# Stage 1's last addition moved to VectorE in iterations with side work, and a changed order of the last outputs and stores

## The chip, the cores and the metric

The kernel runs on one core of a Trainium2 chip. The metric is the device time of one execution in microseconds (us); a comparison uses the median of several runs. Every time in this document is in us unless it is marked ns.

A core has five engines that run their own instruction streams in order and meet through semaphores: TensorE (PE; its weight loads are listed apart as PEld), VectorE (DVE), ScalarE (ACT), GpSimd (POOL) and SyncE (SP). SP does no arithmetic; it issues DMAs, as ScalarE can too.

## The reference

The input `x` has 128 samples of 64 channels and 1024 positions, in float32; `cond_512` holds a style vector of 128 numbers for each sample. Four convolution layers (three taps, 64 to 64 channels) run one after the other, and the result is added to `x`. The weights of every layer are scaled for each sample.

```python
TYPES = ('same', 'upsample', 'same', 'downsample')
...
s = style @ mw.T + mb
weight = SCALE * w * s[:, None, :, None]
demod = lax.rsqrt(jnp.sum(weight * weight, axis=(2, 3)) + EPS)
weight = weight * demod[:, :, None, None]
...
if typ == 'same':
    out = jax.vmap(_conv_same)(x, weight) + b[None, :, None]
elif typ == 'upsample':
    out = jax.vmap(_conv_up)(x, weight.transpose(0, 2, 1, 3)) + b[None, :, None]
    out = _blur(out, 2.0 * blur_k, (1, 1))
elif typ == 'downsample':
    xb = _blur(x, blur_k, (2, 2))
    out = jax.vmap(_conv_down)(xb, weight) + b[None, :, None]
...
x = x + out
```

There is no nonlinear step between the layers, so the four of them are one linear map for each sample.

## The kernel before, in words

The kernel uses that linearity. For each sample it multiplies the weights of the four layers and the blur kernels into one combined kernel, and then convolves `x` once with it. The few positions at both ends of a row, where padding makes the combined kernel wrong, are computed layer by layer in small pieces ("ends").

**Tiling.** Four samples make one quad `q`; 32 quads are the 32 iterations of the main loop (line 1101). 64 channels of two samples fill the 128 partitions, and every matrix product is made of 64 by 64 quarters.

**The weight chain of a quad** has three stages, spread over the iterations ahead of the quad's convolution. In iteration `q` the loop works on four quads at once: outputs of `q`, convolution of `n = q+1`, stages 2 and 3 of `c = q+2`, stage 1 of `s = q+3`.
- Stage 1 multiplies layers 4 and 3 into the tile `S` (six slots of 64 columns for each half). `stage1_a` makes the first matmuls and lets ScalarE copy four slots (L411, shown as L340 of the helper `scaled_copy`). `stage1_b` makes two more groups of matmuls, lets VectorE form slots 4 and 5 (two `scalar_tensor_tensor`, L422), and adds slot 0 onto slot 2 with one `tensor_add` on GpSimd (L425). That addition reads only slots which ScalarE has written.
- Stage 2 multiplies `S` with layer 2 and the blur (`E`), 36 products, L439. Its first four products read slots 1 to 3 of `S`, so they need the addition; slots 4 and 5 are read by the next four.
- Stage 3 multiplies in layer 1 (L480). VectorE then forms sums of the taps (`H`, L501 in the helper `sum_of`).

**The convolution** is done in a form with five products (conv0 to conv4, L590). VectorE forms differences of the input planes (`G` with L501, `T` with L550 and L577), and GpSimd two more (`T`, L565 and L570, 128x684 each). VectorE's `sum1` (the tile `y`) stands ahead of conv2, and its `sum2` (the tile `Y`, then `y`, L641) ahead of the next iteration's conv4. ScalarE writes the outputs (`output`, L659) with a scale and a bias for each half; the six planes of a quad go out by two stores (L664).

**Order.** The schedule is written by hand: the order of the calls in the loop is the order on each engine. An iteration has these calls in this order: stage 2 of `c`; sum2 of `q`; the tap sums of `n`; conv4 of `q`; stage 3 of `c` and conv3 of `n` with the input differences in between; part of conv0; conv1; sum1; the rest of conv0; part of conv2; the rest of conv2; the stores. GpSimd's L565 and L570 for `c` (`in1`, `in2`) stand ahead of sum1.

**Side work.** In iterations 1, 2, 3, 5, 6, 7, 9, 12, 14, 19 and 24 (the dictionary `SLOTS`, L1031) a group of matmuls for the ends or for per-sample constants takes the place at which stage 1 otherwise begins. Stage 1 of `s` is then pushed back: `stage1_a` to where `stage1_b` otherwise stands, and `stage1_b` behind the first part of conv2 (L1206). In those iterations only the second and third part of conv2 lie on PE between `stage1_b` and the next iteration's stage 2. The side work's vector operations (`extra`, L1208) stand directly behind `stage1_b`, ahead of the next iteration's sum2. They are on VectorE and GpSimd, and some follow in iterations that have no such matmuls.

**The last iteration** (L1107 to L1119) has only conv4, the outputs and the stores. For each half it writes three planes: plane 2 (from `Y`), plane 1 (from `y`) and plane 0 (from conv0). `BOTH` is the pair ScalarE, VectorE: plane 1 of half 0 is written by ScalarE, that of half 1 by VectorE, and so for plane 0. The four stores are issued by SP in this order: planes 1 and 2 of half 0, of half 1, plane 0 of half 0, of half 1.

Of the kernel before, what the change touches and what calls it, by code (L numbers as in the profile page):

```python
# [55 lines left out]
K = 3  # L56
# [7 lines left out]
def kernel(  # L64
# [9 lines left out]
    nc = tc.nc  # L74
# [8 lines left out]
    nc_v, nc_a, nc_g = nc.vector, nc.scalar, nc.gpsimd  # L83
# [282 lines left out]
    def tap_matmul(ps, wd, at, n, weight, taps, first=False, last=False):  # L366
        for r, rows in enumerate(HALF):
            for c, cols in enumerate(HALF):
                nc.tensor.matmul(  # L369
                    ps[r][cols, at * C : (at + n) * C],  # L370
                    weight[rows],
                    wd[c if r == 0 else 1 - c][rows, taps],
                    start=first,
                    stop=last,
                    skip_group_check=True,
                )
# [34 lines left out]
            scaled_copy(nc_a, flat(st[r][:, :4]), ps[r][:, : 4 * C], tBn[:, q, r : r + 1])  # L411
        chain[q] = wd, ps, st, t

    def stage1_b(q):

        wd, ps, st, t = chain[q]
        tap_matmul(ps, wd, 1, 1, w2n[:, 3, :], slice(3, 4))
        tap_matmul(ps, wd, 3, 1, w2n[:, 4, :], slice(4, 5), last=True)
        for r in range(2):
            p1 = st[r][:, 0:1, :].to_broadcast([P, 2, C])  # L420
            sums = ps[r][:, C : 5 * C].rearrange("c (a b o) -> c a b o", a=2, b=2)[:, :, 0]
            nc_v.scalar_tensor_tensor(  # L422
                st[r][:, 4:, :], sums, tB[:, q, r : r + 1], p1, op0=ALU.mult, op1=ALU.subtract
            )
        nc_g.tensor_add(t[:, :, 2], t[:, :, 2], t[:, :, 0])  # L425
        chain[q] = st

    def stage2(q, pool=None, engs=(nc_a, nc_a), between=None):
        st = chain[q]
        ps = unit(pool or ps_w, f"psR{q}")  # L430
        for n, e in enumerate((-2, -1, 0, 1, 2, 3, 4, 5, 6)):
            if e % 2 == 0:
                a, lo, m = slice(1, 4), e // 2 + 1, 3
            else:
                a, lo, m = slice(4, 6), (e + 3) // 2, 2
            for r, rows in enumerate(HALF):
                for c, cols in enumerate(HALF):
                    src = st[c if r == 0 else 1 - c]
                    nc.tensor.matmul(  # L439
                        ps[r][cols, lo * C : (lo + m) * C],  # L440
                        E[rows, e + 2, :],
                        src[rows, a, :],
                        start=(n == 0),
                        stop=(n == 8),
                        skip_group_check=True,
                    )
        if between:
            between()
        rt = []
        for r in range(2):  # L450
            t = r_pool.tile([P, 7, C], F32, tag="R", name=f"R{q}_{r}")
            scaled_copy(
                engs[r], t.rearrange("c t o -> c (t o)"), ps[r][:, : 7 * C], tC[:, q, r : r + 1]
            )
            rt.append(t)
        chain[q] = rt
        return ps
# [152 lines left out]
    def banks(q):  # L610
        return A[q] if isinstance(A[q], list) else [A[q][:, s] for s in range(2)]
# [24 lines left out]
    def sum2(q):  # L636
        m3 = m3c.pop(q)
        for s, a in parts(q):
            sum_of(Y[:, s, :NB], m3[:, s], 3.0, a)
        for s, a in parts(q):  # L640
            nc_v.tensor_sub(y1w[q][:, s], y1w[q][:, s], a)  # L641

    def conv4(q, *groups):
        product(q, 4, Y_banks, groups or range(K))

    def conv0(q, *groups):
        product(q, 0, banks(q), groups)
# [3 lines left out]
    def output(q, i, s, eng=nc_a):  # L651

        if q not in os:
            os[q] = opool.tile([P, 2, K, NB], F32, tag="o", name=f"o{q}")
        d3, add = td[:, q, s : s + 1], tb[:, q, s : s + 1]
        src = (banks(q)[s][:, :NB], y1w[q][:, s], Y[:, s, :NB])[i]
        dst = os[q][:, s, i]
        if eng is nc_a:
            nc_a.activation(dst, src, AF.Identity, bias=add, scale=d3)  # L659
        else:  # L660
            eng.tensor_scalar(dst, src, d3, add, op0=ALU.mult, op1=ALU.add)

    def store(q, s, planes=slice(0, K)):
        nc.sync.dma_start(  # L664
            out[q, :, s, planes.start * NB : planes.stop * NB],
            os[q][:, s, planes].rearrange("c i j -> c (i j)"),
        )
# [108 lines left out]
    def zeros():  # L776
        for t in Ye:
            nc_g.memset(t[:, :, 0:1], 0.0)
            nc_g.memset(t[:, :, 7:8], 0.0)
        for t in Ue:  # L780
            nc_g.memset(t[:, :, 0:1], 0.0)
            nc_g.memset(t[:, :, 10:11], 0.0)
        for t in Ve:
            nc_g.memset(t[:, :, 0:2], 0.0)
            nc_g.memset(t[:, :, 10:12], 0.0)
        nc_g.memset(g1, 0.0)
# [142 lines left out]
    BOTH = nc_a, nc_v  # L929
# [171 lines left out]
    for q in range(NQ):  # L1101
        n, c, s = q + 1, q + 2, q + 3
        if q == 1:
            nc.sync.dma_start(Xe, x_ends)
        if q == 5:
            zeros()
        if n == NQ:  # L1107
            conv4(q)
            for i in range(2):
                output(q, 2, i)  # L1110
            for i, eng in enumerate(BOTH):
                output(q, 1, i, eng)
            for i in range(2):
                store(q, i, slice(1, 3))
            conv0(q, *range(K))
            for i, eng in enumerate(BOTH):
                output(q, 0, i, eng)
                store(q, i, slice(0, 1))
            break  # L1119
        if c < NQ:  # L1120
            stage2(c)
        if n < NQ - 1:
            sum2(q)
        if n < NQ - 1:
            combine_a(n)
            combine_b(n)

        if n == NQ - 1:

            conv3(n, ps_w)  # L1130
            copy_m3(n)
            conv4(q, 0, 1)
            for i in range(2):
                output(q, 1, i)
            conv1(n)
            sum1(n)
            conv4(q, 2)
            for i in range(2):
                output(q, 2, i)
            in04(n, 0)  # L1140
            in04(n, 1)
            conv0(q, 0)
            conv2(n)
            conv0(q, 1, 2)
            sum2(n)
            for i in range(2):
                output(q, 0, i)
                store(q, i)
            continue

        conv4(q)
        if q == 0:
            var_matmul(PART[1], var_of(PART[1]), start=False)
            var_root(PART[1], var_of(PART[1]))
            var_inverse(PART[1])
            var_newton(PART[1])
            table_A(PART[1], dm[:, 2, PART[1]])
            for of in (table_C, vector_c0, table_3, vector_Da):
                of(PART[1])
        for i in range(2):  # L1160
            output(q, 2, i)
        if c < NQ:
            stage3(c, 0)
        conv3(n)
        copy_m3(n)
        in04(n, 0)
        in04(n, 1)
        if q:
            in3(c)
            in_g01(c, 0)  # L1170
            in_g01(c, 1)
        if c < NQ:
            stage3(c, 1)
        conv0(q, 0)
        conv1(n, 0)
        if q in SLOTS:
            slot(*SLOTS[q])
        elif s < NQ:
            stage1_a(s)
        conv1(n, 1, 2)  # L1180
        for i in range(2):
            output(q, 1, i)
        if q:
            in_g2(c)
            load(c + NX)
        if q and c < NQ - 1:
            in1(c, nc_g)
            in2(c, nc_g)
        if n == NQ - 2:
            combine_a(n + 1, lambda: sum1(n))  # L1190
            combine_b(n + 1)
        else:
            sum1(n)
        if q == 0:
            in_g01(c, 0)
            in_g01(c, 1)
        conv0(q, 1)
        if q in SLOTS:
            stage1_a(s)
        elif s < NQ:  # L1200
            stage1_b(s)
        conv0(q, 2)
        for i in range(2):
            output(q, 0, i)
        conv2(n, 0)
        if q in SLOTS:  # L1206
            stage1_b(s)
        extra(q, 0)  # L1208
        extra(q, 1)
        if s + 1 < NQ:  # L1210
            scale3(s + 1)
        conv2(n, 1, 2)
        if n == NQ - 2:
            sum2(n)
            in1(n + 1, nc_v)
            in2(n + 1, nc_v)
        if q == 0:
            in_g2(c)
            in3(c)
            load(c + NX)  # L1220
            in1(c, nc_g)
            in2(c, nc_g)
        for i in range(2):
            store(q, i)
# [74 lines left out]
```

## Time and profile before

| | |
|---|---|
| median of 3 runs | 495.94 (495.86 to 497.52) |
| span of the profiled execution | 495.3 |
| mean granted TensorE clock | 0.997 |
| GpSimd's L425, 29 times | 447 to 985 ns, median 463 ns |
| VectorE's L422, 58 times | 340 to 353 ns, median 343 ns |
| GpSimd's L565 and L570, 30 times each | 1668 and 1664 ns, mean |
| last four stores, from issue to landing | 3.4 to 4.3 |

How to read the lines that follow in the prediction. A row of the list of waits is "engine, tile and line that waited <- who ended the wait: total time, how often, longest". A row of the timeline is "start, length, engine, line, operation, out<-in, shape, count", and in brackets the engine's idle time before it and what ended it. Engines with a q behind the name are their sequencers, which issue DMAs. A row of the table by windows is the window, its length, the busy time of each engine with the number of its instructions, the granted clock, the share of the 16 DMA engines that were busy, and GB/s. The profile shows VectorE instructions that follow each other overlapping by up to 0.09.

### The profile page before, as it was taken

What the parts mean: (1) busy time and instruction counts of PE and PEld (TensorE: products, weight loads), DVE (VectorE), ACT (ScalarE), POOL (GpSimd) and SP (SyncE); (2) the same over time, 40 slices, a digit from 0 to 9 for tenths busy, and PEclk for the clock granted to TensorE, in tenths of its full rate; (3) what the DMA queues carried; (4) which work ended last, traced back from release to release, by engine and by line L of the source; (5) the groups of instructions that cost most, each with busy time, mean ns of one, the idle gap of its engine ahead of it and who ended that gap; (6) DMA issues with size and microseconds to landing.
All of it is one profiled execution on the core that took longest, in us unless ns stands there. A gap on an engine that the chain in (4) does not pass through costs nothing.

```text
span 495.3 us, 22221 instructions
## 1 busy us (share of the span) xinstructions
PE 481.3 (97%) x10056; PEld 359.4 (73%) x10056; DVE 396.0 (80%) x692; ACT 290.8 (59%) x580; POOL 142.1 (29%) x175
## 2 busy tenths in 40 slices
PE   8999999999999999999999999999999999999994
PEld 6877767766776766767888777767767778888862
DVE  4986987798888869996768897759998768878782
ACT  5366646557565656555566656656555657566552
POOL 3544423435223222123232122222123333211200
PEclk9999999999999999999999999999999999999998
DMA  7220644442334442354433344442344442434224
GB/s 247 95 90 3 219 167 174 172 162 93 118 148 172 174 148 84 118 171 172 173 127 113 119 161 172 174 146 82 124 167 172 172 161 101 155 129 164 88 86 171
DMA packets 19728, 70.42 MB, mean 142 GB/s; under 512 B 2224, under 2 KB 2992, under 8 KB 19632
## 3 DMA queue, kind: packets, MB, share of 16 engines
q1 hardware_dynamic: 19552, 68.87, 39.0%
q8 instruction: 79, 1.29, 1.1%
q14 instruction: 17, 0.14, 0.1%
q10 hardware_dynamic: 80, 0.11, 0.1%
HBM read 35.36 MB, written 33.62 MB: 139 GB/s over the span
## 4 chain that ended last, share of the span: by engine, by line
PE 78%; DVE 13%; POOL 5%; issue 2%; ACT 0%; POOLq 0%; DVEq 0%
PE psA L590 35%; PE psR L439 13%; PE psW L480 12%; PE Y L590 9%; PE psS L369 5%; DVE G L501 3%; DVE H L501 2%; POOL T L565 2%; POOL T L570 2%; PE psE L820 2%; DVE T L577 2%; DVE Y L501 1%; DVE y L641 1%; POOL S L425 1%; DVE Wf L498 1%
## 5 line engine op out<-in xcount | busy, mean ns | idle before, releaser
L590 PE MATMUL psA<-T,H 64*64 64x340 f32 x2304 | 192.5, 446 | 0.7 <-DVE y L501 0.7
L565 POOL TENSOR_TENSOR T<-G 128x684 f32<-128x684 f32 x30 | 50.0, 1668 | 295.3 <-DVE G L501 268.8
L590 PEld LDWEIGHTS psA<-T,H 64*64 64x64 f32 x2304 | 94.3, 133 | 51.5 <-DVE y L501 5.6
L439 PE MATMUL psR<-S,E 64*64 64x192 f32 (+1 forms) x2304 | 88.1, 300 | 4.7 <-POOL S L425 4.0
L439 PEld LDWEIGHTS psR<-S,E 64*64 64x64 f32 x2304 | 78.4, 133 | 16.9 <-POOL S L425 10.4
L340 ACT ACTIVATE R<-psR,tC 128x448 f32<-128x448 f32 x63 | 36.6, 631 | 75.6 <-PE psR L439 73.8
L501 DVE SCALAR_TENSOR_TENSOR G<-X 128x688 f32<-128x688 f32 (+1 forms) x96 | 78.2, 867 | 0.0
L590 PE MATMUL psA<-T,Wf 64*64 64x340 f32 x768 | 74.4, 447 | 0.0
L501 DVE SCALAR_TENSOR_TENSOR y<-psA,m 128x680 f32<-128x680 f32 (+1 forms) x33 | 27.8, 845 | 48.2 <-PE psA L590 47.0
L340 ACT ACTIVATE Wf<-psW,t 128x384 f32<-128x384 f32 (+1 forms) x126 | 56.4, 498 | 11.2 <-PE psW L480 11.2
L480 PE MATMUL psW<-R,w0s 64*64 64x128 f32 (+1 forms) x1536 | 62.0, 287 | 0.4 <-ACT Wf L340 0.3
L590 PE MATMUL Y<-T,Wf 64*64 64x340 f32 x768 | 61.7, 446 | 0.4 <-DVE Y L501 0.3
L480 PEld LDWEIGHTS psW<-R,w0s 64*64 64x64 f32 x1536 | 51.0, 133 | 8.3 <-ACT Wf L340 1.2
L577 DVE TENSOR_TENSOR T<-G 128x684 f32<-128x684 f32 x64 | 52.7, 865 | 0.0
L659 ACT ACTIVATE o<-Y,tb,td 128x340 f32<-128x340 f32 x64 | 37.2, 631 | 23.7 <-ACT R L340 17.1
L570 POOL TENSOR_TENSOR T<-G 128x684 f32<-128x684 f32 x30 | 49.9, 1664 | 0.0
L369 PEld LDWEIGHTS psS<-wd,w2n 64*64 64x64 f32 x1160 | 38.8, 133 | 10.7
L659 ACT ACTIVATE o<-psA,tb,td 128x340 f32<-128x340 f32 x63 | 36.7, 634 | 14.4 <-PE psA L590 14.4
L590 PEld LDWEIGHTS Y<-T,Wf 64*64 64x64 f32 x768 | 32.4, 133 | 16.6 <-DVE Y L501 1.0
L340 ACT ACTIVATE S<-psS,tBn 128x256 f32<-128x256 f32 x58 | 24.4, 471 | 25.7 <-PE psS L369 25.6
L659 ACT ACTIVATE o<-y,tb,td 128x340 f32<-128x340 f32 x63 | 38.8, 668 | 0.0
L622 ACT COPY m<-psA 128x680 f32<-128x680 f32 (+1 forms) x33 | 23.3, 710 | 25.6 <-PE psA L590 25.6
(147 smaller groups left out, 533.2 us busy)
## 6 DMA issues: line engine op xcount, KB each, us to landing
X<-in_x SPq DMA_DIRECT2D x64, 516.0 KB, 4.4
out<-o SPq DMA_DIRECT2D x62, 510.0 KB, 4.3
out<-o SPq DMA_DIRECT2D x2, 340.0 KB, 3.8
Xe<-in_x_ends SPq DMA_DIRECT2D x1, 512.0 KB, 7.6
par<-in_params SPq DMA_DIRECT2D x2, 192.0 KB, 3.4
out<-o SPq DMA_DIRECT2D x2, 170.0 KB, 3.9
par_s<-in_params_s SPq DMA_DIRECT2D x1, 196.0 KB, 2.8
par<-in_params SPq DMA_DIRECT2D x2, 96.0 KB, 2.9
```

The lines of the kernel that those rows point to most:

```text
L340: nc_a.activation(dst, src, AF.Copy, scale=f)
L369: nc.tensor.matmul(ps[r][cols, at * C : (at + n) * C], weight[rows], wd[c if r == 0 else 1 - c][rows, taps], start=first, stop=last, skip_ ...
L439: nc.tensor.matmul(ps[r][cols, lo * C : (lo + m) * C], E[rows, e + 2, :], src[rows, a, :], start=(n == 0), stop=(n == 8), skip_group_check ...
L480: nc.tensor.matmul(ps[r][cols, at : at + m * C], w0s[kind][rows, k, :], rt[c][rows, first : first + K * (m - 1) + 1 : K, :], start=(n == 1 ...
L501: nc_v.scalar_tensor_tensor(out, x, f, y, op0=ALU.mult, op1=op)
L565: eng.tensor_add(t[:, :, 0, :NJ], plane(g, 2), plane(g, 1))
L570: eng.tensor_sub(t[:, :, 1, :NJ], plane(g, 2), plane(g, 1))
L577: nc_v.tensor_sub(t[:, c, :, :NJ], both(a, PL), both(b, 1))
L590: nc.tensor.matmul(ps[s][cols, :NB], w, Ts[q, tag][rows, c, i, g : g + NB], start=(g == 0 and m == 3), stop=(g == K - 1), skip_group_check ...
L622: nc_a.copy(m3c[q][:, s], a)
L659: nc_a.activation(dst, src, AF.Identity, bias=add, scale=d3)
L820: nc.tensor.matmul(ps[r][cols, : HB * n].rearrange("c (b j) -> c b j", j=n), weight(i, r, c)[rows], moving(i, r, c)[rows], start=(i == 0), ...
```

## The change

Two things are changed, and the arithmetic is the same. First, `stage1_b` takes the engine of its last addition as an argument. In the iterations with side work it is called with VectorE; elsewhere the addition stays on GpSimd. In VectorE's order it stands behind the two L422 of its quad and ahead of the side work. Second, in the last iteration VectorE writes plane 1 of both halves, and the store of plane 0 of half 0 is issued from ScalarE's queue, behind the output that ScalarE writes.

```diff
-    def stage1_b(q):
+    def stage1_b(q, eng=nc_g):
...
-        nc_g.tensor_add(t[:, :, 2], t[:, :, 2], t[:, :, 0])
+        eng.tensor_add(t[:, :, 2], t[:, :, 2], t[:, :, 0])
...
-    def store(q, s, planes=slice(0, K)):
-        nc.sync.dma_start(
+    def store(q, s, planes=slice(0, K), queue=nc.sync):
+        queue.dma_start(
...
-            for i, eng in enumerate(BOTH):
-                output(q, 1, i, eng)
+            for i in range(2):
+                output(q, 1, i, nc_v)
             for i in range(2):
                 store(q, i, slice(1, 3))
             conv0(q, *range(K))
-            for i, eng in enumerate(BOTH):
+            for i, (eng, queue) in enumerate(zip(BOTH, (nc_a, nc.sync))):
                 output(q, 0, i, eng)
-                store(q, i, slice(0, 1))
+                store(q, i, slice(0, 1), queue)
...
         if q in SLOTS:
-            stage1_b(s)
+            stage1_b(s, nc_v)
```

## The prediction

> **What bounds the kernel now.** I read the page first, then the list of waits, then the timeline of each iteration that has side work, the groups' idle times, and at last the DMA of the final microseconds.
>
> ```profile
> PE 481.3 (97%) x10056; PEld 359.4 (73%) x10056; DVE 396.0 (80%) x692; ACT 290.8 (59%) x580; POOL 142.1 (29%) x175
> PEld psR L439 <- POOL S L425: 10.4, 12, 1.4
> PE psR L439 <- POOL S L425: 4.0, 7, 0.8
> ```
>
> TensorE (PE) is busy for 97% of the span, so a change pays only where PE stands still. The largest standstill that this change can touch is the first matmul of stage 2 (L439), which waits for GpSimd's (POOL's) last addition of stage 1 (L425). But most of those waits lie in iterations without side work, where the addition stays on GpSimd. Side work runs in iterations 1, 2, 3, 5, 6, 7, 9, 12, 14, 19 and 24; the timelines show PE waiting for L425 in three of them, 1, 5 and 7:
>
> ```profile
> 62.16 1.65 POOL L570 TENSOR_TENSOR T<-G 128x684 f32<-128x684 f32 x1
> 62.48 0.61 DVE L422 SCALAR_TENSOR_TENSOR S<-psS,tB,S 128x128 f32<-128x128 f32 x2 [1.28 <-PE psS L369]
> 63.01 0.84 DVE L760 TENSOR_TENSOR cc<-raw,a 128x16 f32<-128x16 f32 x1
> 63.76 0.46 POOL L425 TENSOR_TENSOR S<-S 128x128 f32<-128x128 f32 x1
> 64.28 2.73 PE L439 MATMUL psR<-S,E 64*64 64x192 f32 x72 [0.75 <-POOL S L425]
> ...
> 121.62 1.65 POOL L570 TENSOR_TENSOR T<-G 128x684 f32<-128x684 f32 x1
> 122.99 0.40 DVE L760 TENSOR_TENSOR cc<-raw,a 128x96 f32<-128x96 f32 x1
> 123.75 2.73 PE L439 MATMUL psR<-S,E 64*64 64x192 f32 x72 [0.26 <-POOL S L425]
> ...
> 151.09 1.66 POOL L570 TENSOR_TENSOR T<-G 128x684 f32<-128x684 f32 x1
> 152.33 0.96 DVE L800 TENSOR_TENSOR Xm<-Xe,sc 128x512 f32<-128x512 f32 x1
> 152.69 0.91 POOL L425 TENSOR_TENSOR S<-S 128x128 f32<-128x128 f32 x1
> 153.66 2.73 PE L439 MATMUL psR<-S,E 64*64 64x192 f32 x72 [0.82 <-POOL S L425]
> ...
> 79.29 0.20 DVE L760 TENSOR_TENSOR cc<-raw,Da 128x16 f32<-128x16 f32 x1
> ```
>
> In each, the addition stands behind GpSimd's T subtraction (L570). A second reading decides what the move is worth: L760 on 128x16 takes 0.20 in iteration 2 and 0.84 in iteration 1, where it ends at 63.85, just behind L570's end (62.16 + 1.65 = 63.81). A VectorE (DVE) operation with both inputs in SBUF stood still until GpSimd was done. In iteration 7 it goes the other way: L800 had begun, and L425 took 0.91 instead of 0.46.
>
> **The moved addition, its price.** The new DVE instruction is a 128x128 tensor_tensor, placed behind the two L422, where L760 or L800 starts now.
>
> ```profile
> 137.34 0.61 DVE L422 SCALAR_TENSOR_TENSOR S<-psS,tB,S 128x128 f32<-128x128 f32 x2 [1.61 <-PE psS L369]
> 137.86 0.25 DVE L236 TENSOR_TENSOR nw<-dm,var 128x96 f32<-128x96 f32 x1
> 138.19 2.68 PE L439 MATMUL psR<-S,E 64*64 64x192 f32 x72
> 140.66 0.85 DVE L641 TENSOR_TENSOR y<-y,psA 128x680 f32<-128x680 f32 x1
> 140.79 1.33 PEld L590 LDWEIGHTS Y<-T,Wf 64*64 64x64 f32 x21 [0.28 <-DVE Y L501]
> ```
>
> From 96 to 680 elements a tensor_tensor goes from 0.25 to 0.85, 1.03 ns an element, so 128 cost 0.28. Behind the L422 pair the next instruction starts 0.09 before their end (137.86 against 137.95), so of 0.28 about 0.20 is added to VectorE's time.
>
> Iterations 1, 5, 7 (the gain): by L760 in iteration 1 the addition would be held to 63.81, and end at 63.85 + 112 more elements, 0.12, = 63.97; the wait's handover is 0.05 to 0.06 (L425 ends at 64.22, PE starts at 64.28), so PE starts at 64.02, not 64.28: 0.26. Iteration 5: L760 on 96 ends at 123.39, the addition at 123.42, PE at 123.47: 0.28. Iteration 7: L570 ends at 152.75, the addition at 152.91, PE at 152.96: 0.70. Together -1.24. If it were not held, it would end 0.28 behind its start, and PE would start at 63.34, 123.32 and 152.66: -2.37. I take the held value, since a 16-element and a 96-element operation of the same kind stood in that very place. What stood there is then later by little: it was being held, or held up by L425, itself.
>
> The Trainium skill, "SBUF — State Buffer", section "Who interferes with whom", has a rule against this part: a VectorE instruction with two SBUF inputs contends with a GpSimd instruction that reads SBUF, and the one that comes second is blocked for the other's whole length. By the rule the sum is the held one, without it the free one; the 0.84 of L760 agrees with the rule.
>
> The other eight iterations (the cost): there L425 was done in time, and PE starts by its own order. In iteration 6 the addition would end at 137.95 + 0.20 = 138.15, PE could start at 138.20 where it starts at 138.19 now. What is lost is the early weight load: the groups behind a wait take 2.73, this one 2.68. I take 0.06; bounds 0 and 0.28. In iterations 2, 12 and 24 that is all: 0.18.
>
> In the others 0.20 of VectorE time reaches PE, because VectorE does not rest between side work and the next subtractions. First through sum2 (Y, L501), for which conv4 waits:
>
> ```profile
> 95.64 0.85 DVE L501 SCALAR_TENSOR_TENSOR Y<-m,psA 128x680 f32<-128x680 f32 x1
> 96.54 1.95 PE L590 MATMUL Y<-T,Wf 64*64 64x340 f32 x24 [0.35 <-DVE Y L501]
> ...
> 192.28 2.44 DVE L501 SCALAR_TENSOR_TENSOR G<-X 128x688 f32<-128x688 f32 x3
> 196.50 1.65 POOL L570 TENSOR_TENSOR T<-G 128x684 f32<-128x684 f32 x1
> 198.10 0.78 POOL L425 TENSOR_TENSOR S<-S 128x128 f32<-128x128 f32 x1
> 198.94 1.32 PE L439 MATMUL psR<-S,E 64*64 64x192 f32 x32 [0.68 <-POOL S L425]
> ...
> 273.05 0.37 PEld L439 LDWEIGHTS psR<-S,E 64*64 64x64 f32 x12 [0.42 <-POOL S L425]
> 347.30 0.39 PE L439 MATMUL psR<-S,E 64*64 64x192 f32 x4 [0.41 <-POOL S L425]
> 213.31 0.21 PEld L439 LDWEIGHTS psR<-S,E 64*64 64x64 f32 x8 [0.60 <-POOL S L425]
> 287.42 0.21 PEld L439 LDWEIGHTS psR<-S,E 64*64 64x64 f32 x8 [0.59 <-POOL S L425]
> ```
>
> That happens in iteration 3 (the Y of 95.64) and in 6 (Y's weights at 140.79 come 0.04 behind sum2's end). Then through the next iteration: VectorE's G (192.28) ends, GpSimd makes two T of 1.65 and then its L425, and PE waits. After iterations 9, 14 and 19 these are the waits at 198.94, 273.05 and 347.30, and each moves out with G. Five times 0.20: +1.00 (bounds 0, if VectorE finds rest I don't see, and 5 x 0.28 = 1.40).
>
> Part of that comes back. At 213.31 and 287.42 the weights waited 0.60 and 0.59, which cost PE some 0.17 each by the start times of its matmuls; there VectorE follows an earlier point of PE, so a later PE waits less: -0.35 (bounds 0 and -0.35).
>
> The queue behind the moved instruction: on VectorE the side work and sum2, counted above. On GpSimd the side work moves up by 0.46 and nobody waits for it; its two large operations of each iteration wait for G, as before.
>
> What iteration 7 gains is late next at L425 of iteration 8:
>
> ```profile
> 166.77 0.45 POOL L425 TENSOR_TENSOR S<-S 128x128 f32<-128x128 f32 x1
> 167.86 2.35 PE L439 MATMUL psR<-S,E 64*64 64x192 f32 x64
> ```
>
> L425 ends at 167.22, and with the handover PE could start at 167.27, 0.59 earlier than now. Of the 0.70 up to 0.11 is lost again there, unless VectorE, with no L425 beside L800 any more, brings G earlier by as much. I take half, +0.05; whatever more iteration 7 gained would be stopped here.
>
> **The end.** VectorE makes both middle outputs, ScalarE one fewer, and the last small store of half 0 leaves from ScalarE.
>
> ```profile
> 488.29 0.67 ACT L659 ACTIVATE o<-y,tb,td 128x340 f32<-128x340 f32 x1
> 488.93 0.63 DVE L661 TENSOR_SCALAR o<-psA,td,tb 128x340 f32<-128x340 f32 x1 [2.57 <-PE psA L590]
> 490.39 0.76 SPq L664 DMA_DIRECT2D out<-o  x1
> 489.30:489.80 0.50, 0.00 (x0) 0.00 (x0) 0.27 (x1) 0.21 (x1) 0.00 (x0) 1.00 0.09 33
> 489.80:492.60 2.80, 0.00 (x0) 0.00 (x0) 0.00 (x0) 0.00 (x0) 0.00 (x0) 0.89 1.00 371
> 492.60:493.70 1.10, 0.00 (x0) 0.00 (x0) 0.00 (x0) 0.00 (x0) 0.00 (x0) 0.50 0.11 35
> q8 instruction: 1, 0.02, 1.3%
> ```
>
> The output of 488.29 held the first of four stores; now that store can go at about 487.9, and the last at 489.6 (the end of 488.93's row) instead of 490.39. The extra VectorE output falls into its 2.57 of idle time, and costs nothing. So the issue gains 0.79, and the DMA engines' pause of 0.50 (share 0.09) closes. But from 492.60 to 493.70 the share is only 0.11: one or two of 16 engines are late by a microsecond, and those end the kernel. The q8 row (window 486.5 to 493.7) shows why, as I read it: one instruction fetch held one engine for 1.3% of 16 x 7.2, 1.5 us, just before the stores. That engine has had no pause to close. I take -0.1; bounds 0 and -0.8.
>
> The Trainium skill, "DMA: Bandwidth & Descriptors", section "Issuing engines are not separate DMA queues", says that all issuers share the same 16 DMA engines and a second one saves only issue time. By the rule alone the end would gain the issue's 0.79; by the late engine nearly nothing.
>
> **The sum.** -1.24 + 0.05 + 0.18 + 1.00 - 0.35 - 0.1 = -0.5. The profiled span is 495.3 and the median of the runs 495.94, 0.6 above it; 495.3 - 0.5 + 0.6 = 495.4.
>
> **The rivals.** (a) The addition isn't held by GpSimd: -2.37 for -1.24, but iteration 7's 1.00 is cut to 0.69 at 166.77: -1.3 in all, 494.6. For it: an L422, also with an SBUF input, runs freely beside L570; against: L760. (b) The end pays: no late engine, -0.8 for -0.1, 494.7. For it: the pause and the issue times; against: the 0.11 row. (c) Slower: GpSimd's side work, 0.46 earlier in its queue, gets in front of the addition and holds it, as L570 held L760. Held by 0.46 in eight iterations, with PE waiting for each, the 0.18 and 1.00 become 8 x 0.46 = 3.7: +2.0, 497.9. It decides from 0.21 each on, where the sum passes zero (8 x 0.21 = 1.69 = 1.24 + 0.35 + 0.1). Against it: in most of these iterations GpSimd's side work waits for VectorE results that come behind the addition.
>
> **How the numbers follow.** Forecast 0.55, with its own range 494.8 to 496.3 (bounds of the costs: 1.00 to 1.40 and 0.06 to 0.28 upward, regained time and end downward); (a) 0.14, (b) 0.14, (c) 0.13; (a) with (b), with less than 1.00 lost on VectorE, reaches under 493.5: 0.04. The range 494.1 to 497.0 leaves out the last and most of (c). Half a per cent, 2.5 us, is about what a measurement of this kernel can tell from no change: faster 0.08 (the 0.04 and the far half of two gains together), slower 0.05 (the far part of (c)), within it 0.87.
>
> **What would show it.** In iteration 1 the VectorE addition ends near 63.97, held, in place of 63.3; stage 2 starts there some 0.05 later. The waits for POOL at 198.94, 273.05 and 347.30 grow by about 0.2 or stay, and the wait on L425 vanishes from iterations 1, 5 and 7 alone. In the last microsecond few DMA engines are busy though the last issue is at 489.6 less the shift. I am wrong if side work on GpSimd holds the additions of iterations 2 to 24, if PE's waits after 9, 14 and 19 shrink, or if the end gains more than half a microsecond.

## The result and the profile after

The changed kernel took 496.48 (median of 14 runs, 495.49 to 498.24), the kernel before on the same chip 496.17 (14 runs): a ratio of 0.9996 with a 95% interval from 0.9982 to 1.0009. No difference can be told, as forecast; 496.48 lies inside the range, 1.1 above the predicted 495.4.

Executions of one kernel differ by some 3 us, which hides terms of tenths. So two profiled executions are compared here by two stretches. An iteration's stage 2 (L439) means here, as in the prediction, the one that uses the `S` made in that iteration; in the order of calls it opens the next one. The *loop* runs from the first matmul of the stage 2 of iteration 0 to that of iteration 28, the *end* from there to the end of the span. In timelines of TensorE, before:

```profile
48.02 0.55 PE L439 MATMUL psR<-S,E 64*64 64x192 f32 x4
...
462.73 0.48 PE L439 MATMUL psR<-S,E 64*64 64x192 f32 x5
```

and after:

```profile
47.06 0.38 PE L439 MATMUL psR<-S,E 64*64 64x192 f32 x2
...
462.12 0.49 PE L439 MATMUL psR<-S,E 64*64 64x192 f32 x5
```

The loop took 414.71 before (462.73 - 48.02) and 415.06 after, 0.35 more; the end 32.56 (495.29 - 462.73) and 32.60 (494.72 - 462.12). The start came 0.96 earlier in this execution of the changed kernel, and so its span is shorter although loop and end are longer. Its time was 496.51 at a span of 494.7: what lies around the span is 1.8, and 1.8 to 2.1 in the runs of the experiments, not the 0.6 that the prediction worked with. A difference of tenths can be read from the loop, since it repeats: three profiled kernels with the loop of before (before, e2 and e8 below) have 414.67 to 414.71, two with the loop of after (after and e5) 415.06 and 415.10.

The *step* of an iteration is how much later (+) or earlier (-) its stage 2 starts against before, counted from the start of the iteration ahead of it. After the change the steps are:

| iteration | step |
|---|---|
| 1, 5, 7 | -0.17, -0.19, -0.53 |
| 2, 12, 24 | +0.09, +0.10, +0.10 |
| 3, 6 | +0.14, +0.13 |
| 9 and 10, 14 and 15, 19 and 20 | +0.15 +0.09, +0.12 +0.09, +0.10 +0.09 |
| 8, 13, 23, 25 | -0.02, +0.02, +0.02, +0.02 |
| 11, 16 and all others | 0.00, within 0.01 |

The timeline after, around stage 2 of iterations 1, 2, 5 and 7 (start, length, engine, line, operation; in brackets the wait):

```profile
61.22 1.64 POOL L570 TENSOR_TENSOR T<-G 128x684 f32<-128x684 f32 x1
62.06 0.94 DVE L425 TENSOR_TENSOR S<-S 128x128 f32<-128x128 f32 x1
62.93 0.16 DVE L760 TENSOR_TENSOR cc<-raw,a 128x16 f32<-128x16 f32 x1
63.15 2.73 PE L439 MATMUL psR<-S,E 64*64 64x192 f32 x72 [0.58 <-DVE cc L760]
...
77.79 0.28 DVE L425 TENSOR_TENSOR S<-S 128x128 f32<-128x128 f32 x1
77.99 0.35 DVE L227 TENSOR_SCALAR var<-raw 128x384 f32<-128x384 f32 x1
78.19 0.73 PEld L439 LDWEIGHTS psR<-S,E 64*64 64x64 f32 x21 [0.49 <-issue]
78.22 0.89 PE L439 MATMUL psR<-S,E 64*64 64x192 f32 x17
...
120.72 1.66 POOL L570 TENSOR_TENSOR T<-G 128x684 f32<-128x684 f32 x1
122.09 0.43 DVE L425 TENSOR_TENSOR S<-S 128x128 f32<-128x128 f32 x1
122.67 1.10 PE L439 MATMUL psR<-S,E 64*64 64x192 f32 x24
...
150.24 1.64 POOL L570 TENSOR_TENSOR T<-G 128x684 f32<-128x684 f32 x1
151.48 0.55 DVE L425 TENSOR_TENSOR S<-S 128x128 f32<-128x128 f32 x1
152.17 1.10 PE L439 MATMUL psR<-S,E 64*64 64x192 f32 x24 [0.19 <-DVE S L425]
```

The addition on VectorE was held until GpSimd's T was through: in iteration 1 T ends at 62.86 and the addition at 63.00, in iteration 5 at 122.38 and 122.52, in iteration 7 at 151.88 and 152.03. Where T was not running the addition took 0.28, as in iteration 2, and the next VectorE operation began 0.20 behind its start: both are the predicted values. In every iteration TensorE starts 0.14 to 0.15 behind the addition's end (63.00 to 63.15; 78.07 to 78.22). That holds in iteration 2 too, where the next VectorE operation is still running, so the release is L425 and the name L760 in the bracket at 63.15 is only the record that ended last.

The waits after (engine, tile, line <- who ended it: total, times, longest):

```profile
PEld psR L439 <- POOL S L425: 7.6, 11, 1.3
PE psR L439 <- POOL S L425: 2.3, 4, 0.7
PE psR L439 <- DVE S L425: 0.2, 1, 0.2
```

PE's wait for GpSimd's addition fell from 4.0 to 2.3, and yet the loop grew. What was won lay in three iterations; what was paid lay in eleven, most of it outside the list of waits.

### The profile page after: what moved, and what is told of

Its sections match the earlier page's. It is cut to its first block, busy times and chain, and to the rows that moved or that the text cites. A ratio compares the mean times of both kernels' runs of the same rounds, so it can differ in the third digit from the quotient of the medians.

```text
span 494.7 us, 22227 instructions
## 1 busy us (share of the span) xinstructions
PE 481.8 (97%) x10056; PEld 355.1 (72%) x10056; DVE 398.7 (81%) x704; ACT 290.5 (59%) x579; POOL 137.0 (28%) x164
## 4 chain that ended last, share of the span: by engine, by line
PE 82%; DVE 11%; POOL 4%; issue 2%; ACT 1%; POOLq 0%; DVEq 0%
PE psA L590 37%; PE psR L439 14%; PE psW L480 13%; PE Y L590 9%; PE psS L369 5%; DVE G L501 3%; PE psE L820 2%; DVE H L501 2%; POOL T L565 1%; DVE T L577 1%; POOL T L570 1%; PE Y L169 1%; DVE Y L501 1%; DVE y L641 1%; DVE Wf L498 1%
## 5 line engine op out<-in xcount | busy, mean ns | idle before, releaser
L590 PEld LDWEIGHTS psA<-T,H 64*64 64x64 f32 x2304 | 92.8, 133 | 53.0 <-issue 6.7
L439 PE MATMUL psR<-S,E 64*64 64x192 f32 (+1 forms) x2304 | 88.0, 301 | 3.6 <-POOL S L425 2.3
L439 PEld LDWEIGHTS psR<-S,E 64*64 64x64 f32 x2304 | 77.3, 133 | 18.0 <-POOL S L425 7.6
```

The lines of the kernel that those rows point to most:

```text
L439: nc.tensor.matmul(ps[r][cols, lo * C : (lo + m) * C], E[rows, e + 2, :], src[rows, a, :], start=(n == 0), stop=(n == 8), skip_group_check ...
L590: nc.tensor.matmul(ps[s][cols, :NB], w, Ts[q, tag][rows, c, i, g : g + NB], start=(g == 0 and m == 3), stop=(g == K - 1), skip_group_check ...
```

## The experiments

"Old end" below means that the last iteration is as before; a number of runs is given where there were several.

**e1: the addition alone.** Only the addition is moved; old end.

```diff
-            stage1_b(s)
+            stage1_b(s, nc_v)
```

> Only stage 1's addition moves; the last outputs and stores stay as before. The loop is measured from the first matmul of stage 2 in iteration 0 to the one in iteration 28 (414.71 before, 415.06 changed), the end from there to the last instruction (32.56 and 32.61). Theory: the loop is a fixed sequence of waits, so it comes out at 415.06 within 0.05 again, with the same steps (0.17 won at iteration 1, 0.19 at 5, 0.5 at 7, 0.09 to 0.16 lost at 2, 3, 6, 9, 10, 12, 14, 15, 19, 20 and 24), and the end at 32.6. Rival: the 0.35 is scatter between executions; then the steps differ by more than 0.1 from the changed kernel's.

Measured: 496.18, loop 415.60, end 32.29. All steps are within 0.03 of those after the change but one: +0.40 at iteration 13, where TensorE paused around 232.8 with no wait on anything. Without it the loop would be 415.20. So the loop's loss comes from the addition, although both expected values were missed: 415.20 is 0.14 above the loop's, and the end 0.3 below its 32.6.

**e2: the end alone.** All additions stay on GpSimd.

```diff
-            for i, eng in enumerate(BOTH):
-                output(q, 1, i, eng)
+            for i in range(2):
+                output(q, 1, i, nc_v)
...
-                store(q, i, slice(0, 1))
+                store(q, i, slice(0, 1), queue)
```

> Only the last outputs and stores change. Theory: fifteen DMA engines finish some 0.6 earlier after TensorE's last matmul, but the engine that an instruction fetch held finishes at the same time; loop 414.71 within 0.05, end 32.56 within 0.15. Rival: the last stores set the end; end 31.8 to 32.0.

Measured: 497.02, loop 414.67, end 33.04. The end was not better than before but 0.48 worse, outside what either theory expected; the fetch experiments below explain it.

**e3: VectorE's time alone.** The additions stay on GpSimd; in the iterations with side work VectorE adds two slots into a tile that nobody reads, behind the two L422.

```diff
+        if extra_add:
+            nc_v.tensor_add(scr, t[:, :, 1], t[:, :, 0])
```

> GpSimd keeps the addition; VectorE makes another one of the same size in the same place in iterations with side work, into a tile that nobody reads. No TensorE instruction waits for it, so it measures VectorE's time alone. Theory: nothing is lost at 2, 12 and 24; 0.1 to 0.2 at 3 and 6 (through sum2) and at 10, 15 and 20 (through G, GpSimd's T and its addition); loop 415.1 to 415.6. Rival: the loss in the changed kernel is TensorE's wait for VectorE alone; loop 414.7 within 0.1.

Measured: 496.45, loop 415.51, 0.80 more than before. Steps of +0.15 to +0.19 at 4, 15 and 20, and none at 2 and 24: 0.20 of VectorE's time reaches TensorE through the next iteration, and the iterations that only got a new release lose nothing here. The steps expected at 3 and 6 are not there: what iteration 3 loses shows at 4, and at 6 conv4 does start 0.20 later, but iteration 7 takes 0.19 less, since GpSimd's addition now comes ahead of L800 (0.50 long, 0.91 before). At iteration 10 the step is +0.52:

```profile
195.43 0.55 DVE L835 TENSOR_TENSOR Ye<-raw,a 128x384 f32<-128x384 f32 x1
195.51 1.97 POOL L570 TENSOR_TENSOR T<-G 128x684 f32<-128x684 f32 x1
196.01 1.88 DVE L836 TENSOR_TENSOR Ye<-Ye,c 128x384 f32<-128x384 f32 x1
197.43 0.77 POOL L423 TENSOR_TENSOR S<-S 128x128 f32<-128x128 f32 x1
198.26 1.64 PE L439 MATMUL psR<-S,E 64*64 64x192 f32 x40 [1.18 <-POOL S L423]
```

Here VectorE's side work began 0.08 ahead of T, and T waited: 1.97 instead of 1.65. After the change, as before it, the order was the other one:

```profile
195.25 1.65 POOL L570 TENSOR_TENSOR T<-G 128x684 f32<-128x684 f32 x1
195.30 2.01 DVE L835 TENSOR_TENSOR Ye<-raw,a 128x384 f32<-128x384 f32 x1
```

The Trainium skill, "SBUF — State Buffer", section "Who interferes with whom", says that the pair of ports which VectorE and GpSimd share is an exclusive lock, and that issue order decides who blocks. The two orders agree: 2.01 for a VectorE operation that took 0.55 when it came first, and 1.97 for a T of 1.65.

**e4: the addition ahead of the two L422.** It is the same VectorE work in another place, where it meets more of T; old end.

```diff
         tap_matmul(ps, wd, 1, 1, w2n[:, 3, :], slice(3, 4))
         tap_matmul(ps, wd, 3, 1, w2n[:, 4, :], slice(4, 5), last=True)
+        if eng is nc_v:
+            eng.tensor_add(t[:, :, 2], t[:, :, 2], t[:, :, 0])
...
-        eng.tensor_add(t[:, :, 2], t[:, :, 2], t[:, :, 0])
+        if eng is not nc_v:
+            eng.tensor_add(t[:, :, 2], t[:, :, 2], t[:, :, 0])
```

> As the changed loop, but VectorE makes the addition ahead of its two L422, in the 1.6 us in which it waits for TensorE; last outputs and stores as before. Theory (an operation with two SBUF inputs stands still for the whole length of GpSimd's T): in 2, 3, 6, 9, 12, 14, 19 and 24 nothing is lost against before; in 5 and 7 the addition waits for the end of T and holds the L422 back, so stage 2 starts no earlier than before there, within 0.3, and iteration 8 is later; loop 414.5 to 415.6. Rival (no hold): all three waits go for nothing, loop 412.5 to 413.0.

Measured: 496.12, loop 415.07. Lines have moved here: the addition is L417.

```profile
59.53 1.64 POOL L565 TENSOR_TENSOR T<-G 128x684 f32<-128x684 f32 x1 [7.36 <-DVE G L501]
60.24 1.09 DVE L417 TENSOR_TENSOR S<-S 128x128 f32<-128x128 f32 x1
61.14 1.69 POOL L570 TENSOR_TENSOR T<-G 128x684 f32<-128x684 f32 x1
62.29 0.92 PE L439 MATMUL psR<-S,E 64*64 64x192 f32 x20
...
67.85 0.54 PE L480 MATMUL psW<-R,par 64*64 64x128 f32 x10 [0.61 <-issue]
...
120.86 1.63 DVE L417 TENSOR_TENSOR S<-S 128x128 f32<-128x128 f32 x1 [1.03 <-ACT S L337]
...
150.80 1.67 DVE L417 TENSOR_TENSOR S<-S 128x128 f32<-128x128 f32 x1 [1.02 <-ACT S L337]
```

In iteration 1 the addition got in between the two T (the first ends at 61.17, the addition at 61.33), and stage 2 gained 0.95. In iterations 5 and 7 it stood still for nearly all of the second T (1.63 and 1.67), and delayed the L422 behind it: a step of +0.39 at 5, and at 7 only -0.17; +0.24 at 6 and +0.33 at 8 are losses too, the first where none was expected. Iterations 3, 12, 14, 19 and 24 show no step: their 0.10 to 0.15 were due to the addition's place behind the L422. Iteration 2, though, gave 0.82 of iteration 1's gain back, in a pause of TensorE at 67.85 that waits for nothing.

**e5 and e8: the late DMA engine.** The windows over the end after the change (length; busy times by engine with the number of instructions; clock; share of the 16 DMA engines; GB/s):

```profile
486.10:488.70 2.60, 2.12 (x32) 1.00 (x24) 0.40 (x1) 1.62 (x3) 0.00 (x0) 1.00 0.97 381
488.70:489.20 0.50, 0.00 (x0) 0.00 (x0) 0.23 (x1) 0.18 (x1) 0.00 (x0) 1.00 1.04 400
489.20:491.90 2.70, 0.00 (x0) 0.00 (x0) 0.00 (x0) 0.00 (x0) 0.00 (x0) 0.91 0.84 311
491.90:493.10 1.20, 0.00 (x0) 0.00 (x0) 0.00 (x0) 0.00 (x0) 0.00 (x0) 0.50 0.05 17
```

The pause between the stores has closed (share 1.04), but for the last 1.2 a share of 0.05 is left, one engine of 16. An instruction fetch had begun at 485.76 and taken 1.45. Two kernels move TensorE's later instructions 128 places back in their stream, by 32 small matmuls ahead of the loop into a tile that is cleared later, so that this fetch comes at another time: e5 is the changed kernel with it, e8 the kernel before.

```diff
     zeros_to_y(2, 256)
+    zeros_to_y(16, 2)
     zeros_to_y(2, 384)
```

> The whole change, with 32 more small matmuls into an accumulator that is cleared afterwards, at the start of the kernel, so that TensorE's last instruction fetch comes about half a fetch period (3 us) earlier than the stores of the end. Seen from TensorE's last matmul, the changed kernel ends 6.5 later (before: 6.4); the sixteenth engine's part of the last store lands at 5.42 there, the fifteenth at 4.33. Theory (one DMA engine is late by the fetch): the sixteenth comes within 0.3 of the fifteenth, at 4.4 to 4.8, and the kernel ends 5.4 to 5.9 after the last matmul. Rival (the stores themselves, or the store from ScalarE's queue, end late): 6.3 to 6.7 as before.

Measured: 495.96, loop 415.10, end 31.63. The DMA summary of the last 15.2 us has one row for instruction fetches (queue: packets, MB, share); below it are the windows over the end:

```profile
q8 instruction: 1, 0.02, 0.4%
```

```profile
486.50:488.90 2.40, 2.14 (x32) 1.02 (x24) 0.18 (x1) 1.40 (x3) 0.00 (x0) 1.00 1.00 398
488.90:492.90 4.00, 0.00 (x0) 0.00 (x0) 0.45 (x1) 0.40 (x1) 0.00 (x0) 0.78 0.74 275
492.90:493.40 0.50, 0.00 (x0) 0.00 (x0) 0.00 (x0) 0.00 (x0) 0.00 (x0) 0.50 0.00 0
```

The one fetch in there came at 480.65, ahead of the last stores. TensorE's last matmul ended at 488.64, and from 492.90, 4.3 later, nothing is moved any more; after the change it ended at 488.22, and one engine was at work up to 493.1, 4.9 later. The loop's steps are those after the change.

> The kernel before, last outputs and stores as before, with the 32 small matmuls of the run that moved the instruction fetch. It parts the two causes of the shorter end there (5.52 after TensorE's last matmul in place of 6.5): the fetch moved, and the new order of the stores. Theory: each pays only with the other or in part; the fifteenth engine's part lands at 4.9 as before and the sixteenth within 0.3 of it, so the kernel ends 5.9 to 6.1 after the last matmul; the new order is then worth 0.4 to 0.5 where no engine is late, and nothing where one is. Rival: the fetch alone makes the difference, 5.4 to 5.7. Loop 414.7 within 0.1.

Measured: 496.07, loop 414.69, end 32.28. From TensorE's last matmul to the end of the span it is 6.16, just above the theory's 5.9 to 6.1 and far from the rival's 5.4 to 5.7. All kernels, with one trace each, show:

| | fetch beside the last stores | fetch elsewhere |
|---|---|---|
| old end | 6.44 (before), 6.18, 6.26, 6.15, 6.18, 6.48 | 6.16 |
| changed end | 6.51 (after), 6.92 | 5.52, 5.41, 5.53, 5.33 |

So the changed end is worth 0.64 (6.16 - 5.52) where no engine is late, and nothing, or a loss of some tenths, where one is. Moving the fetch alone is worth nothing clear: 6.16 lies among the 6.15 to 6.48 of the old end.

**e6: GpSimd's addition earlier.** In iterations without side work the addition goes right behind ScalarE's copies, ahead of GpSimd's T, on GpSimd as before; old end.

```diff
+        if eng is nc_g:
+            eng.tensor_add(t[:, :, 2], t[:, :, 2], t[:, :, 0])
...
-            stage1_a(s)
+            stage1_a(s, nc_g)
```

> The kernel before, with GpSimd's addition put ahead of GpSimd's two T in the iterations without side work (directly behind ScalarE's copies, which it needs); iterations with side work as before. Theory: stage 2's waits for the addition at 4, 10, 11, 16, 20 and 21 go (0.71, 0.86, 0.18, 0.18, 0.65, 0.73), of which 0.4 comes back at 4 as a wait for sum2, while 1, 5 and 7 keep theirs; loop 411.8 to 413.0. Rival: GpSimd's T, 0.4 later, hold VectorE's side work longer, and sum2 and the next T take over the waits; loop 413.8 to 414.7.

Measured: 495.51, loop 413.99, 0.72 less than before: the rival's band, not the theory's. Steps of -0.72, -0.86 and -0.65 at 4, 10 and 20 are the waits for L425 gone; +1.10 and +0.53 follow at 5 and 23:

```profile
108.29 1.97 PE L439 MATMUL psR<-S,E 64*64 64x192 f32 x52
...
111.08 1.35 PE L590 MATMUL Y<-T,Wf 64*64 64x340 f32 x13 [0.82 <-DVE Y L501]
```

TensorE is sooner at conv4 of the next iteration and there waits for sum2, behind VectorE's side work. That wait was hidden under the other. Of the +0.53 at 23 some 0.25 is a pause of TensorE at 378.77 that waits for nothing, of the kind which e10 explains.

**e7: no addition at all.** The matmul of slot 0 writes slots 0 and 2 in one go, with the same weights and 128 columns in place of 64; nothing is left to add. Old end, 9 runs.

```diff
-        tap_matmul(ps, wd, 0, 1, w2n[:, 1, :], slice(1, 2))
...
+                    ps[r][cols, : 4 * C].rearrange("c (a b o) -> c a b o", a=2, b=2)[:, :, 0],
+                    w2n[rows, 1, :],
+                    wd[c if r == 0 else 1 - c][rows, 1:2, :].to_broadcast([C, 2, C]),
...
-        nc_g.tensor_add(t[:, :, 2], t[:, :, 2], t[:, :, 0])
```

> The kernel before without the addition: the matmul that makes slot 0 of S writes the same product into slot 2 as well (128 columns in place of 64, on TensorE), so the sum arises in the accumulator. Last outputs and stores as before. Theory: all waits for the addition go (5.7 in the profile before, at 1, 4, 5, 7, 10, 11, 16, 20 and 21), some 0.4 comes back as a wait for sum2 at 4, and the wider matmuls cost 0.05 in each of 29 iterations (16 columns-doubled groups by the 0.033 of a 128-column row against 0.027 of a 64-column one): loop 410.5 to 411.5, time 491.8 to 493.2. Rival: the waits only hide VectorE's lateness, which then stops conv4 instead; loop 413 or more.

Measured: 494.65 against 496.58, ratio 0.9956 (0.9938 to 0.9974); loop 412.52, end 32.65. The waits give -0.5 to -0.9 each at 1, 4, 7, 10, 20 and 21, and the 0.4 of sum2 comes back as expected (+0.40 at 5). But the iterations without such a wait pay 0.03 to 0.11 for the wider matmuls, most of them 0.10, twice what was expected, and so the loop missed the expected 410.5 to 411.5 and the time its 491.8 to 493.2. Iteration 2 gives back 0.56 again, in part by a pause of TensorE of 0.25 at 68.16.

**e9: the wide matmul only where PE waits**, GpSimd's addition elsewhere, with the changed end and the shifted fetch; 6 runs.

```diff
+    WIDE = (1, 4, 5, 7, 10, 11, 16, 20, 21)
...
+        if q - 3 not in WIDE:
+            nc_g.tensor_add(t[:, :, 2], t[:, :, 2], t[:, :, 0])
```

> What the runs point to: the wider matmul in place of the addition only in the nine iterations in which stage 2 waited for the addition (1, 4, 5, 7, 10, 11, 16, 20, 21), GpSimd's addition in the others, the new last outputs and stores, and the fetch moved. Theory: the waits go (5.7), 0.45 comes back at 4, nine iterations pay 0.10 each: loop 410.2 to 411.2, end 31.5 to 31.8, ratio to the kernel before 0.988 to 0.992. Rival: the wider matmuls' cost stays with all iterations or the waits move to iterations that waited for nothing; loop 412 or more, ratio 0.993 or above.

Measured: 493.28 against 496.18, ratio 0.994 (0.992 to 0.9959); loop 411.29, end 31.50. The loop is 0.1 above its band, and the ratio lies in the rival's; in the profiled execution the loop also began late, at 50.32 against 46.5 to 48.0 elsewhere, for a reason that was not looked into. The 0.10 is gone from the other iterations, and there is no pause in iteration 2. One wait has moved to iteration 22 (lines are one less here):

```profile
375.29 0.94 PE L438 MATMUL psR<-S,E 64*64 64x192 f32 x20 [0.63 <-POOL S L424]
```

**e10 and e11: two more wide iterations.** In e10 there are also fewer matmuls ahead of the loop; 6 runs.

```diff
-    WIDE = (1, 4, 5, 7, 10, 11, 16, 20, 21)
+    WIDE = (1, 4, 5, 7, 10, 11, 16, 20, 21, 22, 23)
...
-    zeros_to_y(16, 2)
-    zeros_to_y(2, 384)
+    zeros_to_y(12, 2)
```

> As in the kernel with the wider matmul in nine iterations, now also in iterations 22 and 23, and the matmuls that clear psM in front of the loop cut as twelve small ones in place of two wide ones (instead of sixteen small ones besides). Theory: the wait for GpSimd's addition that had moved to iteration 22 (0.8) goes, two more iterations pay 0.1 each for the wider matmul, so the loop from the first to the last stage 2 takes 410.5 to 411.0 (411.29 before this edit). The start is no longer delayed (first matmul of stage 2 of iteration 0 at 47.0 to 48.5), TensorE's instruction fetch is still past before the last stores, so the end stays at 31.4 to 31.9. Time 491.0 to 492.5, ratio to the kernel before 0.989 to 0.993. Rival: the wait moves on again, to iterations 24 to 26, or sum2 takes it over: the loop stays at 411.3 or above and the ratio at 0.993 or above.

Measured: 492.41 against 496.62, ratio 0.9916 (0.9883 to 0.995), but the runs fell apart: 490.86, 490.86 and 491.35 on one hand, 493.46, 495.35 and 495.54 on the other. The profiled one, 495.35, has a loop of 414.79 with one step of +4.25 in iteration 2; without it the loop is 410.54, in the expected band. Stage 2 there:

```profile
62.38 2.69 PE L439 MATMUL psR<-S,E 64*64 64x192 f32 x69
67.34 0.38 PE L439 MATMUL psR<-S,E 64*64 64x192 f32 x2 [2.27 <-issue]
```

TensorE stopped inside a run of matmuls with all operands there. Three readings point to why. First, how many weight loads and matmuls had begun when it stopped, from windows over the start of this kernel, of the one with the addition first (e4), and of the one without addition (e7; the counts of matmuls and of weight loads come first):

```profile
0.00:67.30 67.30, 62.02 (x1369) 50.07 (x1370) 53.04 (x110) 36.44 (x82) 29.45 (x59) 1.00 0.45 150
```

```profile
0.00:67.80 67.80, 64.41 (x1369) 50.95 (x1370) 54.70 (x112) 38.14 (x85) 29.20 (x59) 1.00 0.44 149
```

```profile
0.00:68.10 68.10, 64.39 (x1370) 50.70 (x1370) 52.62 (x109) 37.71 (x85) 28.77 (x58) 1.00 0.45 149
```

Three programs with different code stop at the same count, 2739 or 2740; with the semaphore instructions of TensorE's queue it is 2753 in all three. The pause in e1, at 232.8, stands at 9665. The difference is 6912, 27 times 256 to the last instruction, and a fetch moves 16 KB: blocks of 256 instructions, of 64 bytes if a fetch holds one block. Second, a fetch landed shortly ahead of each end of a pause: at 65.96 for 67.34 here, 66.33 for 67.85, 66.78 for 68.16, 231.46 for 232.87. That is 1.4 to 1.5 each time. The rule holds beyond these four: counted in steps of 256 from the same place, no block of TensorE's instructions in any of the 13 traces begins less than 1.2 behind the landing of its fetch, and the pause of e6 at 378.77, 51 blocks behind 2753, ends 1.2 behind one. Third, the clock behind the pause:

```profile
67.30:67.80 0.50, 0.46 (x10) 0.46 (x13) 0.50 (x2) 0.00 (x0) 0.00 (x0) 1.00 0.06 24
67.80:68.20 0.40, 0.40 (x12) 0.35 (x8) 0.40 (x1) 0.28 (x1) 0.00 (x0) 0.89 0.05 20
68.20:68.60 0.40, 0.40 (x9) 0.25 (x4) 0.40 (x2) 0.35 (x1) 0.00 (x0) 0.50 0.25 72
...
69.50:71.50 2.00, 2.00 (x29) 1.81 (x25) 2.00 (x3) 0.47 (x1) 0.00 (x0) 0.50 0.00 0
71.50:73.00 1.50, 1.50 (x47) 1.45 (x42) 0.97 (x2) 1.03 (x3) 0.36 (x1) 0.99 0.00 0
```

So TensorE had run out of instructions, and of the 4.25 some 2.3 are the pause and most of the rest half the clock from 68.1 (0.89 is the mean of 0.40 with full clock for 0.31) to 71.5. e11 tests this by 12 more small matmuls ahead of the loop and nothing else, which moves the boundary by 48 instructions; 6 runs.

```diff
-    zeros_to_y(12, 2)
+    zeros_to_y(18, 2)
```

> As the kernel with the wider matmul in eleven iterations, but the small matmuls in front of the loop are 36 instead of 24, which pushes every later TensorE instruction 48 places back in its stream, and nothing else. Theory: the pause of 2.3 in stage 2 of iteration 1 (and the 0.9 and 0.25 in two kernels before) is TensorE out of instructions, at a boundary of 256 instructions whose fetch came late among the X loads; with the boundary moved to where it lay in the kernel with nine iterations, the fetch is done in time. Step 1 to 2 comes back to -0.1 to 0.1 from +4.25, the loop is 410.4 to 410.9, the end 31.3 to 31.9; all runs lie at 490.4 to 492.3, median 490.8 to 491.5, ratio 0.987 to 0.991. Rival: the pause belongs to that place in the program or comes by chance: step 1 to 2 is +0.5 or more again, or a third of the runs is above 493 as before (three of six were), ratio 0.991 to 0.994.

Measured: 491.24 against 496.13, ratio 0.9911 (0.9887 to 0.9935); loop 410.59, end 31.44, step -0.05 in iteration 2. The pause is gone and the median is in its expected band, but two of the six runs, 492.49 and 493.57, lie above the band for all runs, so the rest of the scatter is not explained. That the moved boundary took the pause away is not shown: the fastest runs of e10, 490.86, can hardly have had a loss of 4.25 either, so the one profiled execution of e11 may have been without it by chance, and one run above 493 against three of six is too few to tell. The fetch of that block, and stage 2:

```profile
q8 instruction: 1, 0.02, 5.2%
```

```profile
62.48 2.80 PE L439 MATMUL psR<-S,E 64*64 64x192 f32 x72
```

The q8 row is of the window 59.5 to 60.6: the fetch began at 59.57, where it began at 65.04 in e10. By the median e11 is the fastest of all, some 0.9% below the kernel before (its ratio can't be told from e10's); its chain of waits is TensorE for 94% of the span.

## Why the prediction was right, and where its sum was not

That nothing measurable would change was right, and so was the mechanism in the main: a gain in three iterations, paid back by VectorE's time, and an end that a late DMA engine keeps. The time is a weak test of it, since anything within a microsecond or two would have looked the same; the sum itself had the wrong sign, -0.5 against +0.4 in the profiles. By term, against the steps of the profiled execution:

| term of the sum | predicted | measured |
|---|---|---|
| gain at 1, 5, 7 | -1.24 | -0.89 |
| given back at 8 | +0.05 | -0.02 |
| late weight load at 2, 12, 24 | +0.18 | +0.29 |
| VectorE's 0.20 in five places (3, 6, 9 with 10, 14 with 15, 19 with 20) | +1.00 | +0.91 |
| regained at 11 and 16 | -0.35 | 0.00 |
| small steps at 13, 23 and 25 | none | +0.06 |
| the end | -0.10 | +0.04 |
| sum | -0.5 | +0.4 |

- **The hold.** Rival (a), an addition that is free of GpSimd, is out: 0.94, 0.43 and 0.55 where T was running, 0.28 in the eight other iterations, and with the addition first a full hold of 1.63 and 1.67.
- **The handover was mis-sized.** The prediction took 0.05 to 0.06 from GpSimd's row; it is 0.14 to 0.15 behind VectorE. A semaphore instruction of 51 ns in TensorE's queue, ahead of stage 2's first weight load, waits for VectorE. Before, it was done 0.4 or more ahead of the first matmul, and the weight load itself waited for GpSimd. Now it ends the wait: in iteration 2 it stands between the addition's end (78.07) and the weights (78.19), and in all eleven iterations it begins 0.11 ahead of the first matmul. That explains some 0.27 of the 0.35 missing at 1, 5 and 7 (3 x 0.09), and the 0.10 instead of 0.06 at 2, 12 and 24. In iteration 7 the rest is that T itself began 0.10 later behind iteration 6's stage 2 (13.00 instead of 12.90), which is VectorE's time from iteration 6.
- **VectorE's time** came out near its size. e3, which has nothing but that time, shows it one iteration further on, with nearly the same sums: 0.15 at 4 against 0.14 at 3 after the change, 0.19 at 15 against 0.21 at 14 and 15, 0.19 at 20 against 0.19 at 19 and 20. So the later release at 3, 14 and 19 adds little; it lets the loss show earlier (e4 has no step there).
- **The regained 0.35 is the step that failed.** The prediction said that "there VectorE follows an earlier point of PE, so a later PE waits less". But VectorE's side work in iteration 10 is itself held by T (L835 at 195.30, 2.01 long) and T follows VectorE's G; so VectorE, GpSimd and TensorE are late together, by 0.24 each from iteration 10's stage 2 to iteration 11's and by 0.21 from 15 to 16, and no wait shrinks. After the change the weights still wait 0.59 in both places:

```profile
212.04 0.21 PEld L439 LDWEIGHTS psR<-S,E 64*64 64x64 f32 x8 [0.59 <-POOL S L425]
286.48 0.21 PEld L439 LDWEIGHTS psR<-S,E 64*64 64x64 f32 x8 [0.59 <-POOL S L425]
```

- **The end.** The prediction gave the pause between the stores little worth because one engine was already late. e5 and e8 show that this was right and why: without the fetch beside the last stores the changed end is worth 0.64, with it nothing. Rival (b) had nearly the size (0.8) and lacked its condition.
- **Rival (c)**, GpSimd's side work in front of the addition, did not occur: no addition outside 1, 5 and 7 took more than 0.28.
- **The number.** 495.4 was the median of three runs less 0.5. The 14 runs put the kernel before at 496.17, 0.2 higher, and the sum's error of 0.9 is about the rest of the 1.1. That loop and end grew by 0.4 is seen in the profiles; the times of the runs alone can't show it.

## What to carry to other kernels

Where two engines hold each other up, look which instructions of the other engine run in the very window to which work is moved: the addition went to a free engine and was held to the same moment by the neighbour it had stood behind. Then ask whether the wait has to be moved at all: the sum could be had from the matmul that made it, only in the iterations that wait. And when TensorE pauses with no wait, or one DMA engine ends late for no store's sake, see whether the stop lies a multiple of 256 instructions from another one, and when the last fetch landed, before blaming the schedule.

## What the runs showed of the hardware that was not expected

- TensorE can run out of code inside a dense loop: pauses of 0.2 to 2.3 at boundaries of 256 instructions, which ended 1.2 to 1.5 behind the landing of a 16 KB fetch. In e10 the DMA engines were busy with loads and stores around that fetch (share 1.01 from 64 to 66), in e11 it ran ahead of them. That the traffic made it late is argued, not shown: the trace has no time at which a fetch is asked for.
- A fetch beside the last stores makes one of the 16 engines late by about a microsecond, and with the changed end the whole kernel with it: 6.5 to 6.9 behind the last matmul instead of 5.3 to 5.5.
- After the pause of 2.3 in e10, which ended at 67.34, the granted clock stayed full to 68.1, then was 0.50 to 71.5. The Trainium skill, "TensorE: Matmul & The Clock Gate", section "What's actually happening", gives an idle window of about 3.4 us as the condition for the slow state. The length of the slow stretch, 3.4, agrees with such a window, but here a pause shorter than one was enough; the pauses of 0.9 and less left the clock at 1.00.
- The wider matmul, 128 columns in place of 64 for eight rows of the trace an iteration, costs 0.10 by most of e7's steps (0.03 to 0.11).
